# Four graph layers on one core: x transposed through DRAM and VectorE blocks instead of TensorE, products that run in either TensorE tile mode, and a new order

## The chip, the cores and the metric

The kernel runs on one core of one Trainium2 chip. The metric is the device time of one launch, in microseconds (us). Three runs of the kernel before took 2814.39, 2812.9 and 2817.28 us, so the median is 2814.39 us. Engines are named as the profile names them: PE is TensorE (its weight loads are PEld), DVE is VectorE, ACT is ScalarE, POOL is GpSimd and SP is SyncE. A small q behind a name (SPq, POOLq) is the engine's own instruction queue, from which DMAs are issued.

## What is computed

There are 32 independent graphs. Each has 512 nodes with 256 features (x) and a dense 512 x 512 adjacency (adj). Four layers follow each other, each with a residual and a layer norm. All arithmetic is float32.

```python
# layer 0: two-layer MLP on the aggregated neighbours
h = (1 + eps) * x + adj @ x
x = layernorm(x + relu(h @ W1 + b1) @ W2 + b2)
# layer 1: graph attention, 4 heads of 64, edges where adj > 0.5
h = x @ W                                    # [n, heads, 64]
e = leaky_relu(e_dst[i] + e_src[j], 0.2), masked
x = layernorm(x + softmax(e) @ h + bias)
# layer 2: 8 heads of 32, scores weighted by adj
q, k, v = x @ Wq.T, x @ Wk.T, x @ Wv.T
x = layernorm(x + softmax(q k^T / sqrt(32) + log(adj + 1e-6)) @ v @ Wo.T + bo)
# layer 3: bilinear similarity, one head
x = layernorm(x + softmax((x @ W) x^T * adj, masked) @ x)
```

## The kernel before

`fast_path` writes the whole computation as named **steps** and lets a small planner put them in order. `prepare()` makes the steps for the weights, `graph(g)` those of one graph, several hundred of them. A step has an engine, an expected duration, the steps it follows, the buffers it takes, and for TensorE a tile mode: "" (the whole array), "row" (32 rows at a time), "c32" (four column strips of 32), "r64". `Plan.order` is a list scheduler. It keeps one time line for each engine, adds `CHANGE[mode]` when a TensorE step has another mode than the step before it, and picks the ready step with the earliest due time. Due times come from a period per graph and from a long table of shifts per step name (the arguments of `plan.run`, under `tc.manual_schedule()`). What comes out is one fixed order of instructions for each engine; on the chip every engine works through its own list and waits on semaphores. The list of a graph in the middle is the same for each graph, shifted by one period, and about four to five graphs are under way at a time, each in another layer.

DMAs are steps too. A step on SP or POOL issues the transfer, a second step occupies a planned transfer queue, and a third adds the landing time. The planner has separate queues for the transfers issued from SP ("q1") and those issued from POOL ("qa"); in it the two do not touch each other.

**Buffers** are shared pools of SBUF tiles: 13 large ones ("B"), 12 of 2 x 512 floats in each partition ("C"), 10 strips ("D"), and 8 PSUM banks ("p"). The tokens L0 to L3 limit how many graphs may be inside a layer (1, 2, 2 and 1).

The steps that matter here, with their lines in the profile:

- Layer 0: `h` (L812) aggregates neighbours, `f` (L835) and `y` (L854) are the two products of the MLP. The adjacency of every graph but the first is loaded already cut into 32 x 32 blocks by four DMAs from SP (L719, tile `Ar`, 128-byte pieces), and DVE then transposes the blocks (L778). So a transpose through DMA and DVE is in use for adj already.
- `residual_steps` adds a product to x and takes the statistics (DVE, L681, L624, L625); `norm_steps` finishes the layer norm: POOL raises the variance to -0.5 (L647), DVE makes the shift (L655), and ACT scales (steps `r1` to `r4`, L670).
- Layers 1, 2 and 3 begin with **x transposed** (features first): for each of two halves TensorE makes four 128 x 128 transposes into a PSUM bank (L882 for layer 1, L1147 in `features_first` for layers 2 and 3), and ACT copies the bank into SBUF (L886, which also sums each feature over the nodes, and L1151).
- Layer 1 then has `v1` (L903), the attention weights on ACT and DVE (L1010, L1021), the products `o1` in mode c32 (L1043), the denominators (L1081) and the small transposes `yt` (L1110, L1111).
- Layer 2 has `q` and `k` (L1166), `v2` (L1184), the scores `s` in mode row (L1203), exponentials on ACT (L1216), their weighting on DVE (L1225) and `n` in mode c32 (L1261). To sum the denominators, POOL issues accumulating DMAs that add one 1 MB tile of weights to another (`collect`, L1236, steps `cd`, six a graph, and two half-size ones, L1289, step `fd`). The product `d2` (L1308, mode r64) needs the last of them; `p` (L1385) is the output product.
- Layer 3 has `i` (L1412), `t` (L1427) and `w` (L1456).
- `bias_steps` (L611) lets POOL add the biases to x by an accumulating DMA of 512 KB, three a graph. At layers 1 and 2 it comes after the transposes that read x.

Of the kernel before, what the change touches and what calls it, by code (L numbers as in the profile page):

```python
# [16 lines left out]
P = 128  # L17
# [6 lines left out]
H1 = 4  # L24
# [24 lines left out]
class Plan:  # L49
# [12 lines left out]

    CHANGE = {"": 0.207, "row": 0.218, "c32": 0.143, "c64": 0.161, "r64": 0.166}
# [69 lines left out]
    def order(self, period, ahead, window, stay, rush=(), moves=(), edges=(0, (), 0, ())):  # L133


        room = {b: [(0.0, i) for i in range(n)] for b, n in self.stock.items()}
        engine, mode, out, last = {}, "", [], 0.0
        held = [{} for _ in self.steps]
        ends = [{} for _ in self.steps]
        waits = [{n: len(s.after) for n, s in steps.items()} for steps in self.steps]  # L140
        fwaits = [[len(after) for _, after in frees] for frees in self.frees]
        ready, low, opened = {}, 0, 0
        todo = [len(steps) for steps in self.steps]
        moved = dict.fromkeys((n for steps in self.steps for n in steps), 0.0)
        turn = [max(g - 1, 0) for g in range(len(self.steps))]
        for i, early in enumerate(rush):
            turn[-1 - i] -= early
        for n, far in moves:
            moved[n] += far
        lead, tail = edges[0], len(self.steps) - edges[2]  # L150
        early, late = dict(edges[1]), dict(edges[3])

        def shift(g, name):
            return moved[name] + (early if g <= lead else late if g >= tail else {}).get(name, 0.0)

        def near(low):
            fill, until, between, left, drain = ahead
            return fill if low < until else drain if low >= len(self.steps) - left else between

        def open_to(n):  # L160
            nonlocal opened
            while opened < min(n, len(self.steps)):
                for name in self.steps[opened]:
                    if not waits[opened][name]:
                        ready[opened, name] = self.ready(opened, name, ends)
                opened += 1

        open_to(window)
        while low < len(self.steps):
            found = []  # L170
            for (g, name), t in ready.items():
                s = self.steps[g][name]
                t = max(t, engine.get(s.eng, 0.0))
                change = self.CHANGE[s.mode] if s.eng == "pe" and s.mode != mode else 0.0
                for k, (kind, _, rest) in enumerate(s.take):
                    r, n = room[kind], sum(b[0] == kind for b in s.take[:k])
                    if len(r) <= rest + n:
                        break
                    t = max(t, r[n][0])
                else:  # L180
                    due = turn[g] * period - self.left[g][name] + shift(g, name) + stay * change
                    found.append((t, due, g, name, change))
            if not found:
                return math.inf, out
            first = min(found)[0] + near(low)
            _, t, g, name, change = min((due, t, *f) for t, due, *f in found if t <= first)
            s = self.steps[g][name]
            t += change
            if s.eng == "pe":
                mode = s.mode  # L190
            del ready[g, name]
            got = {}
            for kind, key, _ in s.take:
                got[key] = held[g][key] = (kind, room[kind].pop(0)[1])
            if s.eng:
                engine[s.eng] = t + s.us
            end = ends[g][name] = t + s.us
            last = max(last, end)
            out.append((g, name, t, got))
            for h, n in s.then:  # L200
                waits[h][n] -= 1
                if not waits[h][n] and h < opened:
                    ready[h, n] = self.ready(h, n, ends)
            for k in s.frees:
                fwaits[g][k] -= 1
                if not fwaits[g][k]:
                    key, after = self.frees[g][k]
                    kind, i = held[g].pop(key)
                    free = max(ends[g][a] + self.HOP.get(self.steps[g][a].eng, 0.0) for a in after)
                    room[kind].append((free, i))  # L210
                    room[kind].sort()
            todo[g] -= 1
            while low < len(self.steps) and not todo[low]:
                low += 1
                open_to(low + window)
        return last, out

    def run(self, tries):

        self.link()  # L220
        best = min((self.order(*t)[0], t) for t in tries)
        assert best[0] < math.inf
        for g, name, _, got in self.order(*best[1])[1]:
            self.slot[g].update((key, i) for key, (_, i) in got.items())
            self.steps[g][name].emit()
# [3 lines left out]
def fast_path(  # L229
# [103 lines left out]


# [249 lines left out]
    def graph(g):  # L584
        plan.graph()
        slot = plan.slot[-1]
        last = g == B - 1
        t = {"g": g}
# [86 lines left out]
        def residual_steps(n, c2, after, free):  # L675


            @step(f"x{n}{c2}", "dve", 0.6, after + prev(f"x{n}", c2), free=(free,))
            def _(c2=c2):
                pair = t["x"][:, 2 * c2 : 2 * c2 + 2, :]  # L680
                nc.vector.tensor_add(pair, pair, t[f"py{c2}"])  # L681
                if c2 == 0:
                    norm_tiles(n)

            for j in range(2):

                @step(f"st{n}{2*c2+j}", "dve", 0.55, (f"x{n}{c2}",))
                def _(c=2 * c2 + j):
                    norm_stats(n, c)

# [133 lines left out]
        for f in range(HC):  # L824
# [3 lines left out]
                take=(f"p=f{f}",) + (() if f else ("B=h1T/2",)),  # L828
            )
            def _(f=f):  # L830
# [3 lines left out]
                for d in range(DC):  # L834
                    nc.tensor.matmul(  # L835
                        ph, w1_sb[:, d, blk(f)], t["hT"][:, d, :], start=(d == 0), stop=(d == DC - 1)
                    )
# [30 lines left out]
        for d in range(DC):  # L868

            @step(  # L870
                f"xt1{d}", "pe", 0.437, row("r1", NC) + prev("xt1", d),
                take=(f"p=xt1{d}",) + (() if d else ("L1", "C=xT1/1")),
            )
            def _(d=d):
                if d == 0:
                    t["xT"] = mid("xT1", [P, DC, N], "xT1")

                    t["R"] = little([P, H1 * NC + DC], "R")
                    t["xs"] = t["R"][:, H1 * NC :]
                pt = t[f"pt{d}"] = bank(f"xt1{d}", [P, N], f"xT1_t_{d}")  # L880
                for c in range(NC):
                    nc.tensor.transpose(pt[:, blk(c)], t["x"][:, c, blk(d)], ident)  # L882

            @step(f"xe1{d}", "act", 0.75, (f"xt1{d}",), free=(f"xt1{d}",))
            def _(d=d):
                nc.scalar.activation(  # L886
                    t["xT"][:, d, :], t[f"pt{d}"], AF.Copy, accum_out=t["xs"][:, d : d + 1]
                )

        bias_steps(2, row("xt1", DC))  # L890

        for c in range(NC):
# [5 lines left out]
            def _(c=c):  # L898
# [3 lines left out]
                for d in range(DC):  # L902
                    nc.tensor.matmul(  # L903
                        pv, t["xT"][:, d, blk(c)], wg_sb[:, d, :], start=(d == 0), stop=(d == DC - 1)
# [6 lines left out]
        plan.free("xT1", row("v1", NC))  # L911
# [10 lines left out]
        @step("R", "act", 0.14, ("ab",))  # L922
# [15 lines left out]
        @step("Rt", "pe", 0.11, ("R",), take=("p=Rt",))  # L938
# [214 lines left out]
        features_first(2, ("L2",))  # L1153
        bias_steps(3, row("xt2", DC))

        def proj(n, o):
            @step(
                f"{n}{o}", "pe", 1.72, row("xe2", DC) + prev(n, o) + (f"^we{n}",),
                take=(f"p={n}{o}",) + (() if o else (f"C={n}",)),
            )  # L1160
            def _():
# [3 lines left out]
                for d in range(DC):  # L1165
                    nc.tensor.matmul(  # L1166
                        pq, wT[n][:, d, blk(o)], t["xT2"][:, d, :], start=(d == 0), stop=(d == DC - 1)
                    )
# [231 lines left out]
        features_first(3, ("L3",), src="x3")  # L1400
        for o in range(DC):
# [3 lines left out]
                take=(f"p=i{o}",) + (() if o else ("C=iT",)),  # L1405
            )
            def _(o=o):
# [3 lines left out]
                for d in range(DC):  # L1411
                    nc.tensor.matmul(  # L1412
                        pq, w3_sb[:, d, blk(o)], t["xT3"][:, d, :], start=(d == 0), stop=(d == DC - 1)
                    )
# [6 lines left out]
        for c in range(NC):  # L1421

            @step(f"t{c}", "pe", 1.72, row("ie", DC) + prev("t", c), take=(f"p=t{c}",))
            def _(c=c):
                pt = t[f"pt{c}"] = bank(f"t{c}", [P, N], f"s3_{c}")
                for d in range(DC):
                    nc.tensor.matmul(  # L1427
                        pt, t["xT3"][:, d, blk(c)], t["iT"][:, d, :],
                        start=(d == 0), stop=(d == DC - 1),
                    )  # L1430
# [567 lines left out]
```

## Time and profile before

| What | us |
|---|---|
| median of three runs | 2814.39 |
| the profiled execution, its own time | 2813.72 |
| its span, first to last instruction | 2812.0 |
| PE busy | 2777.1 |
| DVE busy | 2235.4 |
| ACT busy | 1774.5 |
| POOL busy | 450.9 |
| mean granted TensorE clock | 0.997 of full speed |

The profile counts an engine as busy while it executes; issuing a DMA or waiting is not busy. The line "PE" counts modelled ends of matmuls, so that a busy PE can still have gaps for a change of tile mode. The chain of waits follows the work that ended last back to what released it. Of DMA queues, q0 carries what POOL issues (the accumulating transfers) and q1 what SP issues; both run on the same 16 DMA engines. "To landing" is the time from the issue to the semaphore that says that all data has arrived.

These are the groups that the change removes or touches, as the profile lists them (busy us, mean ns of one | idle time before them):

```profile
L1147 PE MATMUL xT_t<-ident,x 128*128 128x128 f32 x512 | 73.2, 275 | 4.3 <-ACT x L670 4.2
L1151 ACT COPY xT<-xT_t 128x512 f32<-128x512 f32 x128 | 72.8, 597 | 97.9 <-PE xT_t L1147 97.9
L882 PE MATMUL xT_t<-ident,x 128*128 128x128 f32 x256 | 33.6, 273 | 0.0
L886 ACT ACTIVATE xT<-xT_t 128x512 f32<-128x512 f32 x64 | 38.6, 630 | 0.0
```

There are 768 transposes of x by TensorE, 24 for each graph, and six copies by ACT for each graph.

### The profile page before, as it was taken

What the parts mean: (1) busy time and instruction counts of PE and PEld (TensorE: products, weight loads), DVE (VectorE), ACT (ScalarE), POOL (GpSimd) and SP (SyncE); (2) the same over time, 40 slices, a digit from 0 to 9 for tenths busy, and PEclk for the clock granted to TensorE, in tenths of its full rate; (3) what the DMA queues carried; (4) which work ended last, traced back from release to release, by engine and by line L of the source; (5) the groups of instructions that cost most, each with busy time, mean ns of one, the idle gap of its engine ahead of it and who ended that gap; (6) DMA issues with size and microseconds to landing.
All of it is one profiled execution on the core that took longest, in us unless ns stands there. A gap on an engine that the chain in (4) does not pass through costs nothing.

```text
span 2812.0 us, 41564 instructions
## 1 busy us (share of the span) xinstructions
PE 2777.1 (99%) x15540; PEld 1549.1 (55%) x15540; DVE 2235.4 (79%) x4139; ACT 1774.5 (63%) x3438; POOL 450.9 (16%) x526
## 2 busy tenths in 40 slices
PE   8999999999999999999999999999999999999998
PEld 6544565555555555555555655555555555555544
DVE  3878779877779877788877788777798777887785
ACT  3767566676666675666665666766666756666564
POOL 1111111111111111111111111111111111111110
PEclk9999999999999999999999999999999999999999
DMA  8476777667787667786677776667776677667650
GB/s 172 90 160 123 154 143 155 134 137 145 145 158 145 131 139 146 139 171 134 137 141 148 143 160 133 135 143 149 153 144 135 139 146 143 136 134 137 135 104 16
DMA packets 350055, 388.74 MB, mean 138 GB/s; under 512 B 265036, under 2 KB 304920, under 8 KB 317976
## 3 DMA queue, kind: packets, MB, share of 16 engines
q0 software_dynamic: 45568, 277.89, 51.2%
q1 hardware_dynamic: 303296, 107.86, 17.3%
q8 instruction: 124, 2.03, 0.3%
q14 instruction: 83, 0.68, 0.1%
q10 hardware_dynamic: 984, 0.28, 0.0%
HBM read 141.38 MB, written 17.08 MB: 56 GB/s over the span
## 4 chain that ended last, share of the span: by engine, by line
PE 92%; DVE 3%; DMA 2%; ACT 2%; issue 1%; POOL 0%; ACTq 0%; SPq 0%; DVEq 0%; POOLq 0%
PE s L1203 9%; PE hT_ps L812 8%; PE o_ps L1261 8%; PE o_ps L1043 8%; PE h1T_ps L835 8%; PE s L1427 8%; PE o_ps L1456 7%; PE y_ps L854 7%; PE v_ps L903 4%; PE iT_ps L1412 4%; PE qT_ps L1166 4%; PE v_ps L1184 4%; PE o2p_ps L1385 4%; PE kT_ps L1166 4%; PE xT_t L1147 2%; DMA z<-z 1%
## 5 line engine op out<-in xcount | busy, mean ns | idle before, releaser
L1216 ACT ACTIVATE z<-s 128x512 f32<-128x512 f32 x1024 | 535.5, 605 | 214.4 <-PE s L1203 208.1
L1225 DVE SCALAR_TENSOR_TENSOR z<-AT,z 128x1024 f32<-128x1024 f32 x512 | 601.3, 1213 | 13.0 <-ACT z L1216 12.6
L1236 POOL DMA_DIRECT2D z<-z x186 | 164.1, 889 | 1686.2 <-DVE z L1225 522.8
L1351 DVE RECIPROCAL rdT<-rdT 128x256 f32<-128x256 f32 x128 | 214.3, 1721 | 229.2 <-ACT rdT L1344 229.2
L1010 ACT ACTIVATE z<-R_bc,nT,S 128x512 f32<-128x512 f32 x512 | 372.6, 814 | 3.3 <-DMA R_bc<-R_dram 3.2
L1021 DVE SCALAR_TENSOR_TENSOR z<-z,T,edge 128x512 f32<-128x512 f32 x512 | 347.4, 745 | 16.4 <-ACT z L1010 16.2
L670 ACT ACTIVATE x<-x,shift,rstd 128x256 f32<-128x256 f32 x508 | 264.0, 591 | 75.9 <-DVE shift L655 74.6
L1203 PE MATMUL s<-qT,kT 32*128 32x512 f32 x2048 | 288.9, 633 | 0.4 <-ACT kT L1172 0.4
L1261 PE MATMUL o_ps<-z,v 128*32 128x512 f32 x2048 | 264.2, 600 | 3.1 <-DVE z L1225 2.1
L1456 PE MATMUL o_ps<-x,z 128*128 128x257 f32 x1024 | 240.3, 386 | 3.2 <-ACT z L1216 2.5
L1071 DVE TENSOR_TENSOR z<-z 128x1024 f32<-128x1024 f32 (+1 forms) x256 | 237.0, 951 | 4.2 <-PE o_ps L1043 2.7
L1043 PE MATMUL o_ps<-z,v 128*32 128x512 f32 x2048 | 237.2, 599 | 0.0
L835 PE MATMUL h1T_ps<-hT,w_sb 128*128 128x512 f32 x512 | 234.3, 599 | 0.0
L1456 PEld LDWEIGHTS o_ps<-x,z 128*128 128x128 f32 x1024 | 189.2, 189 | 77.9 <-issue 46.3
L1427 PE MATMUL s<-iT,xT 128*128 128x512 f32 x512 | 229.3, 599 | 0.0
L854 PE MATMUL y_ps<-w_sb,h1T 128*128 128x256 f32 x1024 | 226.6, 379 | 0.0
L624 DVE BATCH_NORM_STATS2 st<-x 128x6 f32<-128x256 f32 x508 | 211.5, 416 | 9.3
L812 PE MATMUL hT_ps<-AT,x 128*128 128x384 f32 (+2 forms) x768 | 210.7, 384 | 0.5 <-ACT AT L761 0.5
L854 PEld LDWEIGHTS y_ps<-w_sb,h1T 128*128 128x128 f32 x1024 | 194.0, 190 | 27.4 <-ACT z L1216 0.8
L647 POOL TENSOR_TENSOR rstd<-ve,nhalf 128x4 f32<-128x4 f32 (+1 forms) x131 | 141.1, 1077 | 356.8 <-DVE ve L641 347.7
L841 ACT ACTIVATE h1T<-h1T_ps,b_sb 128x512 f32<-128x512 f32 x128 | 87.9, 687 | 147.7 <-PE h1T_ps L835 147.7
L1203 PEld LDWEIGHTS s<-qT,kT 32*128 32x128 f32 x2048 | 88.7, 183 | 160.8 <-issue 74.1
(162 smaller groups left out, 3763.2 us busy)
## 6 DMA issues: line engine op xcount, KB each, us to landing
z<-z POOLq DMA_DIRECT2D x186, 1024.0 KB, 8.2
x<-biases POOLq DMA_DIRECT2D x96, 512.0 KB, 9.6
R_bc<-R_dram SPq DMA_DIRECT2D x32, 1024.0 KB, 4.6
Ar<-in_adj_dram SPq DMA_DIRECT2D x124, 256.0 KB, 7.5
z<-z POOLq DMA_DIRECT2D x62, 512.0 KB, 7.0
x<-in_x_dram SPq DMA_DIRECT2D x32, 512.0 KB, 9.0
out_dram<-x SPq DMA_DIRECT2D x31, 512.0 KB, 4.1
xs_row<-xs_dram SPq DMA_DIRECT2D x32, 128.0 KB, 5.6
```

The costliest lines, as they stand in the source:

```text
L812: nc.tensor.matmul(ph[:, cols], t["x"][:, m, blk(d)], moving, start=(k == 0), stop=(k == len(parts) - 1),)
L835: nc.tensor.matmul(ph, w1_sb[:, d, blk(f)], t["hT"][:, d, :], start=(d == 0), stop=(d == DC - 1))
L854: nc.tensor.matmul(py[:, j, :], t["h1T"][:, f, blk(2 * c2 + j)], w2_sb[:, f, :], start=(f == 0), stop=(f == HC - 1),)
L1010: nc.scalar.activation(t[f"e{h}"][:, c, :], t["Rbc"][:, h, :], AF.Relu, bias=t["nT"][:, h, c : c + 1], scale=t["S"][:, h, c : c + 1],)
L1021: nc.vector.scalar_tensor_tensor(z, z, t["T"][:, h, c : c + 1], t["edge"][:, c, :], op0=ALU.add, op1=ALU.mult)
L1043: nc.tensor.matmul(po[32 * q : 32 * q + 32, :], t["v"][:, c, hp * P + 32 * q : hp * P + 32 * q + 32], t[f"e{2*hp+q//2}"][:, c, :], start=( ...
L1203: nc.tensor.matmul(pk, t["k"][hs, o, blk(c)], t["q"][hs, o, :], start=True, stop=True)
L1216: nc.scalar.activation(t[f"E{k}"][:, j, :], t[f"ps{k}{j}"], AF.Exp, scale=QSCALE)
L1225: nc.vector.scalar_tensor_tensor(z, t["AT"][:, c, None, :].to_broadcast([P, 2, N]), ADJ_EPS, z, op0=ALU.add, op1=ALU.mult,)
L1261: nc.tensor.matmul(t[f"n{o}"][32 * j : 32 * j + 32, :], t["v2"][:, c, o * P + F2 * j : o * P + F2 * (j + 1)], t[f"E{k}"][:, j, :], start=( ...
L1427: nc.tensor.matmul(pt, t["xT3"][:, d, blk(c)], t["iT"][:, d, :], start=(d == 0), stop=(d == DC - 1),)
L1456: nc.tensor.matmul(py, t[f"z3{m}"][:, blk(c)], t["x3"][:, m, :], start=(m == 0), stop=(m == NC - 1),)
```

## The change

For 27 of the 32 graphs (all but graphs 0, 1, 29, 30 and 31, `near`), the transposes of x by TensorE and, at layers 2 and 3, the copies by ACT are gone. In their place `turned` does this at each of layers 1, 2 and 3: SP writes x (512 KB) to a scratch tensor in DRAM, waits until it has landed, and reads it back with four DMAs of 128 KB in 128-byte pieces, so that the 32 x 32 blocks stand where the transposed x wants them; DVE then transposes the blocks (two instructions of 128 x 512). At layer 1 the sums over nodes, which came with ACT's copy, are made by two ACT passes over the transposed tile (`xa`). The accumulating bias DMA of layers 1 and 2 now waits for the write to DRAM, which reads x.

The 512-column products `f`, `q`, `k`, `i` and `t` get the mode "any". The planner runs such a step in the mode that TensorE is in if that is "" or c32, and in c32 otherwise; `product` then issues either one matmul of 128 columns of weights or four of 32 columns. The order of all steps is searched anew, with a new period and new shifts.

```diff
+    EITHER = {"": "", "c32": "c32"}
...
+                into = self.EITHER.get(mode, "c32") if s.mode == "any" else s.mode
+                change = self.CHANGE[into] if s.eng == "pe" and into != mode else 0.0
...
+    def product(out, lhsT, rhs, start, stop):
+
+        if plan.mode != "c32":
+            nc.tensor.matmul(out, lhsT, rhs, start=start, stop=stop)
+            return
+        for q in range(4):
+            part = slice(32 * q, 32 * q + 32)
+            nc.tensor.matmul(out[part, :], lhsT[:, part], rhs, start=start, stop=stop)
...
+        near = g < 2 or g >= B - 3
...
+        def turned(n, more, src):
+
+            @step(f"xw{n}i", "sp", 0.45, row(f"r{n}", NC))
+            def _():
+                t[f"xd{n}"] = dram.tile([N, D], F32, tag=f"x{n}_dram", name=f"x{n}_dram_{g}")
+                nc.sync.dma_start(t[f"xd{n}"].rearrange("(c p) d -> p c d", p=P), t[src][:, :, :D])
+
+            transfer(f"xw{n}", 2.0, (f"xw{n}i",), land=2.5)
+
+            for a in range(4):
+
+                @step(
+                    f"xl{n}{a}i", "sp", 0.5, (f"xl{n}{a-1}i",) if a else (f"xw{n}",),
+                    take=() if a else (f"C=xL{n}/{2 if n == 1 else 1}",) + more,
+                )
+                def _(a=a):
+                    if a == 0:
+                        t[f"xL{n}"] = mid(f"xL{n}", [P, DC, N], f"xL{n}")
+                    nc.sync.dma_start(
+                        t[f"xL{n}"][32 * a : 32 * a + 32].rearrange("j d (b i) -> j d b i", i=32),
+                        bass.AP(
+                            t[f"xd{n}"].tensor, t[f"xd{n}"].offset + 32 * a,
+                            [[D, 32], [P, DC], [32 * D, N // 32], [1, 32]],
+                        ),
+                    )
+
+                transfer(f"xl{n}{a}", 1.0, (f"xl{n}{a}i",), land=3.0)
+
+            for d in range(DC):
+
+                @step(
+                    f"xe{n}{d}", "dve", 0.6, row(f"xl{n}", 4) + prev(f"xe{n}", d),
+                    take=() if d else (f"C=xT{n}",),
+                )
+                def _(d=d):
+                    if d == 0:
+                        t[f"xT{n}"] = mid(f"xT{n}", [P, DC, N], f"xT{n}")
+                    nc.vector.transpose(t[f"xT{n}"][:, d, :], t[f"xL{n}"][:, d, :])
+
+            plan.free(f"xL{n}", row(f"xe{n}", DC))
...
-        features_first(2, ("L2",))
-        bias_steps(3, row("xt2", DC))
+        if near:
+
+            features_first(2, ("L2",))
+            bias_steps(3, row("xt2", DC))
+
+        else:
+
+            turned(2, ("L2",), "x")
+            bias_steps(3, ("xw2",))
...
                 f"{n}{o}", "pe", 1.72, row("xe2", DC) + prev(n, o) + (f"^we{n}",),
-                take=(f"p={n}{o}",) + (() if o else (f"C={n}",)),
+                take=(f"p={n}{o}",) + (() if o else (f"C={n}",)), mode="any",
```

Layers 1 and 3 are treated like layer 2 (`turned(1, ("L1",), "x")` and `turned(3, ("L3",), "x3")`).

## The prediction

> **What bounds the kernel now.** I read the page first: busy shares, queues, the chain by engine.
>
> ```profile
> PE 2777.1 (99%) x15540; PEld 1549.1 (55%) x15540; DVE 2235.4 (79%) x4139; ACT 1774.5 (63%) x3438; POOL 450.9 (16%) x526
> ...
> q0 software_dynamic: 45568, 277.89, 51.2%
> q1 hardware_dynamic: 303296, 107.86, 17.3%
> ...
> PE 92%; DVE 3%; DMA 2%; ACT 2%; issue 1%; POOL 0%; ACTq 0%; SPq 0%; DVEq 0%; POOLq 0%
> ```
>
> TensorE bounds it: 92% of the chain. Nothing else is full, but VectorE is at 79% and the DMA engines at 51 + 17%. Then one period (a graph in the middle; columns are the stretch, its length, busy PE, PEld, DVE, ACT, POOL, clock, DMA share, GB/s):
>
> ```profile
> 1085.26:1170.52 85.26, 85.26 (x486) 47.92 (x485) 69.52 (x129) 55.02 (x108) 13.81 (x16) 1.00 0.72 145
> ```
>
> A graph costs 85.26 us: DVE works 69.5, ACT 55.0, the DMA engines 0.72 x 85.3 = 61. Then the chain in order of time (start, length, what), for the price of TensorE's parts:
>
> ```profile
> 1433.15 1.72 PE kT_ps L1166 x4
> 1434.87 0.87 PE xT_t L882 x8
> 1435.74 3.46 PE v_ps L1184 x16
> ...
> 1491.13 1.07 PE s L1203 x8
> 1492.20 1.00 PE o_ps L1261 x8
> ...
> 1494.07 3.63 PE h1T_ps L835 x8
> ```
>
> Eight transposes take 0.87 us, so one takes 0.109. A product of 512 columns is two records of 0.43, and 16 records of L1261 (four strips) take the same 1.72 elsewhere in this chain. After a change of mode, 8 records of L1203 take 1.07 where 8 x 0.107 = 0.86 is work: "row" costs 0.21 to enter, c32 0.14 (1.00 - 0.86), the whole array 0.19 (3.63 against 3.44 without a change).
>
> Last, how q1's small pieces fare. Packets, MB and share of the 16 engines: 1 us with q1 alone, then 6 us in which a load of `Ar` (issued at 2537.2) stands beside one collect (issued at 2536.2):
>
> ```profile
> q1 hardware_dynamic: 1428, 0.18, 115.7%
> ```
> ```profile
> q0 software_dynamic: 128, 1.05, 97.1%
> q1 hardware_dynamic: 36, 0.02, 1.4%
> ```
>
> Alone, q1 moves 1428 pieces of 128 bytes in a us. Beside a collect it all but stops: 36 packets in 6 us. From 2267 to 2271 the two queues take turns exactly, 102 packets of 8 KB against 103 of q1. A small piece waits for an 8 KB packet of the other queue every time.
>
> **What the Trainium skill says.** "TensorEngine Tiling (Array Packing)", Key Properties: a change of tiling mode drains the engine. The trace agrees: 0.14 to 0.21 us each. "DMA: Bandwidth & Descriptors", Queues, rings and completion order: each DMA engine goes round its queue rows packet by packet. The trace agrees (102 against 103), and shows what that means when one packet is 64 times the other. Same page, Two DMAs through the same engine are not ordered: a read of what an earlier DMA wrote must wait for its semaphore; so SP's wait between write and reads is real and holds SP's queue. "VectorE: DVE Perf Modes", The three transpose paths: VectorE transposes 32 x 32 blocks only, hence the DMA that places blocks; L778 has the same shape, 0.67 us.
>
> **The change part by part.** Sums are against the profiled execution, 2813.7 us, 0.7 below the median.
>
> *TensorE work removed.* 27 graphs x 24 transposes x 0.109 = 70.6 us. Counting modes in the two built orders, changes fall from 717 to 536: 92 fewer into the whole array (x 0.19), 44 into row (x 0.21), 45 into c32 (x 0.14): 17.5 + 9.2 + 6.3 = 33.0. Products in strips cost nothing more (1.72 either way); 0 to 0.02 per load group of four, I take 0. All of it is on the path: 103.6 us, giving 2710. That is 3.8 a graph.
>
> *ACT.* Four copies of 0.597 a graph go; the two of layer 1 become `xa`. ACT is at 65%: worth 0.
>
> *DVE.* Six block transposes of 0.67 are 4.0 a graph: 73.5 of 81.4, 90%. Covered by TensorE while their input is there; they also stop whatever is queued behind them while it is not.
>
> *DMA.* Per graph 12,288 pieces at 13 ns of one engine (115.7% x 16 us / 1428) = 10.0 us of all sixteen, and 1,536 of 1 KB (375 in 1.5 us at 96%: 61 ns) = 5.9. 61 becomes 77, that is 94% of 81.4. Nothing hides a late one: TensorE's list is fixed.
>
> *The time that each layer leaves.* I laid measured lengths along TensorE's built list and read off the work between producer and user.
>
> Layer 1. From the end of `y` (call it Y) to `v1` the list holds 24.3 us. In the trace before, the last copy of r1 ends at Y + 8.3, so the write is issued then. On DVE the last weighting (L1225, 1.2) before collect c7 (step cd7; c5 and c6 likewise) stands directly after r1's shift, r1's four copies (2.4) end 1.2 later: c7 is issued about Y + 7.2, its packets run from +1.4 (its usual delay) for 5.7, to Y + 14.3. The write gets turns only, then needs 24 of its 32 packets per engine alone (512 take 2.05 us, so 1.5), and 0.8 to land: L = Y + 16.6. At L both SP and POOL go on: four reads on q1, and on q0 the bias DMA (2.8) directly followed by collect c6 (5.4), which stands next in POOL's list. The reads' first quarter gets through, the rest waits to L + 9.7, then 3072 pieces take 2.6, landing 0.8, DVE 1.4: Y + 31.3. TensorE waits 31.3 - 24.3 = 7.0. From both sides: without rivalry the write takes 3.6, the reads 5.7 (1.4 to start, 3.5, 0.8), DVE 1.4: Y + 19, no wait; with nothing let through, 8.
>
> Layer 3. `p` to `i` holds 37.4, r3 is ready at 18.6 (ten us of L1021 stand before its shift on DVE). The write lies beside c5 and a half collect, 7.6; the reads share q1 with the next graph's `Ar`, 10,240 pieces, 1.4 + 8.9 + 0.8; DVE 1.4. 38.7 against 37.4: about 1, of which half shifts `v1` as well: 0.5 (0 to 3).
>
> Layer 2. `yt` to `q` holds 23.1; r2 takes 9.5, SP's queue is full of layer 3's reads until about 11.6, the write lands at 13.9, reads beside a bias DMA end at 20 to 22.5, DVE 1.4. 0 to 1; I take 0.
>
> Waits: 7.5 a graph x 27 = 202. Forecast 2710 + 202 = 2912. Behind the waiting transposes DVE holds layer 2's weightings and the reciprocals for `p`; with 15 us idle a period it makes that up.
>
> **Rivals.**
>
> *The DMAs hide* (ends faster). The saved 3.8 a graph stays, only layer 3's wait of about 1 counts: 2710 + 27 x 1.1 = 2740. It holds if the reads of layer 1 are not caught behind c6, for which 5.7 instead of 13.1 us is enough: Y + 24 against 24.3. For it: TensorE waited only some 50 us in all before (2797 from first to last matmul, 2745 of work and changes), and the same device works for `Ar`. Against it: `Ar` has a whole period of room, and lands in 3.9 to 17.0 us. Decided at a wait of 3.8 a graph.
>
> *Half caught.* A collect issued into running `Ar` traffic had its first packet 2.1 to 3.9 us after issue, not 1.4. If that delay lets most of the reads pass, the wait is about 2.5 + 0.5: 2710 + 81 = 2791.
>
> *DMA as the bound.* At 94% the waits of layers 2 and 3 come to 2 or 3 each and late collects keep buffers: 12 a graph, 3034.
>
> That the transposes do not leave is excluded: 648 fewer stand in the built list.
>
> **How the numbers follow.** About 0.2% (5.6 us) is what can be told from no change. Forecast (2850 to 2970): 0.48. Hidden (2700 to 2775): 0.29. Half caught (2775 to 2850): 0.15, split 0.06 faster, 0.04 same, 0.05 slower. Bound (over 2970): 0.08. Faster 0.35, same 0.04, slower 0.61. Both signs are likely, so the range reaches from most of "hidden" to the top of the forecast: 2728 to 2965, leaving out 0.09 below and 0.10 above. The forecast's own range is 2850 to 2970.
>
> **What would show it.** PE groups for transposes of x down to 120 instructions; busy PE minus waits near 2700; DMA share per period near 0.85; PE waits at `v_ps` of layer 1 (released by ACT or DVE behind the reads) of some 7 us a graph; reads of layer 1 landing 10 us or more after issue, of layer 2 in about half that. It is wrong if those reads land in 6 us, or if TensorE's waits gather at another step.

## The result, and the profile after

The changed kernel takes 3065.81 us (median of 4 runs, 3063.36 to 3073.78) against 2813.64 us before: a ratio of 1.090, interval 1.0877 to 1.0923. It is 252 us slower. The forecast, 2912, had the direction and the place, but its range ended at 2965, and the loss is 2.6 times the 98 us that it meant.

From the page of the changed kernel: busy time by engine, the queues, the chain by engine.

```profile
PE 2765.9 (90%) x18576; PEld 1472.5 (48%) x18576; DVE 2319.2 (76%) x4301; ACT 1731.0 (56%) x3330; POOL 475.0 (16%) x526
...
q0 software_dynamic: 45568, 277.89, 48.4%
q1 hardware_dynamic: 683024, 192.82, 28.2%
...
PE 33%; DMA 26%; DVE 24%; SPq 7%; ACT 6%; issue 2%; POOL 2%; DVEq 0%; ACTq 0%; POOLq 0%
```

TensorE's share of the chain fell from 92% to 33%; transfers and VectorE stand there now. Its busy time fell by only 11 us, though 104 us of work left its list. Both are clues: it waits, and some of what it does takes longer.

Where it waits, from the list of waits (waiting instruction, what came last, us in all, times, longest):

```profile
PE v_ps L978 <- DVE xT L740: 179.9, 24, 9.9
PE s L1284 <- ACT qT L1253: 17.2, 24, 0.9
PE d_ps L1156 <- DVE rd_all L1549: 12.1, 23, 0.9
```

The first is the wait that was forecast, `v1` behind the layer-1 reads, 7.5 us each. The other two were not in my sum.

The chain in order of time around one such wait; in this period `y` ends at 1546.6, so `v1` starts at Y + 32.9:

```profile
1554.60 2.08 ACT x L682 x4
...
1556.70 8.03 DMA x_dram<-x
...
1564.88 0.56 SPq L721
...
1568.15 10.34 DMA xL<-x_dram
...
1578.68 0.72 DVE xT L740
...
1579.54 6.66 PE v_ps L978 x16
```

The write takes 8.0 us (8.3 forecast), and from the issue of the first read to VectorE's start it is 13.8 (from the write's landing on, 13.1 forecast). What the reads meet can be counted: packets of the two queues, MB and share of the 16 engines, from 1572 to 1575:

```profile
q0 software_dynamic: 78, 0.64, 102.0%
q1 hardware_dynamic: 78, 0.01, 4.4%
```

For each of c6's packets of 8 KB one piece of 128 bytes gets through; beside the bias DMA, which comes in packets of 4 KB, it is much the same (42 against 41 from 1568.5 to 1569.5).

The last line of the chain is new: 16 matmul records of `v1` take 6.66 us; before the change they took 3.76. The windows say why (stretch, length, busy PE, PEld, DVE, ACT, POOL, clock, DMA share, GB/s): the whole period, the wait, and `v1` itself.

```profile
1546.60:1641.10 94.50, 85.61 (x595) 45.67 (x594) 73.58 (x136) 53.67 (x103) 14.94 (x16) 0.95 0.83 167
1571.50:1579.50 8.00, 1.09 (x6) 0.61 (x4) 0.81 (x2) 2.35 (x5) 0.82 (x1) 0.72 0.97 205
1579.50:1586.20 6.70, 6.66 (x17) 5.28 (x18) 6.01 (x8) 1.99 (x6) 0.00 (x0) 0.56 0.78 158
```

This period is 94.50 us long, where it was 85.26. During the wait the DMA engines are at 97%, and TensorE's granted clock falls to half and stays there through most of `v1` (0.56). Over the whole run the clock stood at half for 276 us, before the change for 18.

### The profile page after: what moved, and what is told of

Its sections match the earlier page's. It is cut to its first block, busy times and chain, and to the rows that moved or that the text cites. A ratio compares the mean times of both kernels' runs of the same rounds, so it can differ in the third digit from the quotient of the medians.

```text
span 3063.9 us, 48491 instructions
## 1 busy us (share of the span) xinstructions
PE 2765.9 (90%) x18576; PEld 1472.5 (48%) x18576; DVE 2319.2 (76%) x4301; ACT 1731.0 (56%) x3330; POOL 475.0 (16%) x526
## 4 chain that ended last, share of the span: by engine, by line
PE 33%; DMA 26%; DVE 24%; SPq 7%; ACT 6%; issue 2%; POOL 2%; DVEq 0%; ACTq 0%; POOLq 0%
DMA xL<-x_dram 13%; DMA x_dram<-x 12%; DVE z L1096 9%; PE v_ps L978 5%; SPq L721 4%; PE hT_ps L867 4%; PE o_ps L1342 4%; PE s L1284 4%; DVE z L1306 3%; DVE z L1146 3%; ACT x L682 3%; DVE st L636 2%; SPq L774 2%; PE v_ps L1265 2%; PE o2p_ps L1466 2%
## 5 line engine op out<-in xcount | busy, mean ns | idle before, releaser
L1306 DVE SCALAR_TENSOR_TENSOR z<-AT,z 128x1024 f32<-128x1024 f32 x512 | 610.1, 1214 | 130.6 <-ACT z L1297 130.4
L740 DVE STREAM_TRANSPOSE xT<-xL 128x512 f32<-128x512 f32 x162 | 106.2, 691 | 330.0 <-DMA xL<-x_dram 308.7
L978 PE MATMUL v_ps<-wg_sb,xT 128*128 128x264 f32 x512 | 174.3, 510 | 182.7 <-DVE xT L740 179.9
L1317 POOL DMA_DIRECT2D z<-z x186 | 171.0, 919 | 1042.9 <-PE o_ps L1342 587.0
L659 POOL TENSOR_TENSOR rstd<-ve,nhalf 128x4 f32<-128x4 f32 (+1 forms) x131 | 166.8, 1275 | 686.3 <-DVE ve L653 634.2
L1342 PE MATMUL o_ps<-z,v 128*32 128x512 f32 x2048 | 251.6, 596 | 7.5 <-DVE z L1306 7.4
L1118 PE MATMUL o_ps<-z,v 128*32 128x512 f32 x2048 | 241.9, 603 | 6.8 <-ACT z L1297 4.3
L978 PEld LDWEIGHTS v_ps<-wg_sb,xT 128*128 128x128 f32 x512 | 130.2, 262 | 228.0 <-issue 189.7
L1539 PE MATMUL o_ps<-x,z 128*128 128x257 f32 x1024 | 233.5, 380 | 2.4 <-ACT z L1526 2.4
L1146 DVE TENSOR_TENSOR z<-z 128x512 f32<-128x512 f32 (+1 forms) x256 | 231.1, 953 | 1.6
L344 PE MATMUL s<-iT,xT 128*32 128x512 f32 x1840 | 210.3, 594 | 0.0
```

Source lines behind the costliest of these rows:

```text
L978: nc.tensor.matmul(pv, t["xT1"][:, d, blk(c)], wg_sb[:, d, :], start=(d == 0), stop=(d == DC - 1))
L1146: nc.vector.tensor_add(z[:, :m, :], z[:, :m, :], z[:, m : 2 * m, :])
L1306: nc.vector.scalar_tensor_tensor(z, t["AT"][:, c, None, :].to_broadcast([P, 2, N]), ADJ_EPS, z, op0=ALU.add, op1=ALU.mult,)
L1342: nc.tensor.matmul(t[f"n{o}"][32 * j : 32 * j + 32, :], t["v2"][:, c, o * P + F2 * j : o * P + F2 * (j + 1)], t[f"E{k}"][:, j, :], start=( ...
L1539: nc.tensor.matmul(py, t[f"z3{m}"][:, blk(c)], t["x3"][:, m, :], start=(m == 0), stop=(m == NC - 1),)
```

## The experiments

Theory A: the layer-1 reads starve beside the large packets of POOL's queue, and TensorE's wait for them, with the slow clock behind it, is the loss. Rivals: the traffic of all three trips is the loss; the new order or the strips are.

**Layer 2 alone, planned anew.** `TURN` holds only 2; the line is put in likewise for layers 2 and 3.

```diff
-        if near:
+        if near or 1 not in TURN:
```

> Only layer 2 goes through DRAM; layers 1 and 3 are transposed on TensorE as before, products in either mode, order planned anew by the same rules. The built list of TensorE is shorter than before's by 216 transposes (23.5 us) and 122 mode changes (23.4 us): 47 us. The list holds 27 us between the last transpose of y and the first product on the turned x, and the trip of layer 2 took 22 to 23 us. Theory A (the loss is the wait for layer 1's reads, plus what it drags behind it): no wait of size is left, the clock stays at 1.00: 2813 - 47 = about 2767 (2755 to 2785). Rival B (the new order or the products in strips cost time by themselves): no faster than 2813, and product groups longer than 0.43 us a pair of records. Rival C (any DRAM trip delays the engine): waits at q or k of 3 us or more a graph, 2800 to 2850.

Measured: 3552.5 us, ratio 1.264 (1.2618 to 1.266). None of the theories. The shifts of due times had been fitted to another set of steps, and I take the order that came out to be poor in many places; no run shows that by itself. The two largest of its waits:

```profile
PE hT_ps L869 <- issue: 113.1, 18, 6.3
PE xT_t L939 <- ACT x L684: 65.3, 76, 3.3
```

Neither has to do with layer 2's trip, which TensorE waited for only 15.4 us in 24 graphs. It tells nothing on the change, except that a shorter built list isn't a faster kernel. In all further kernels the order of the kernel after (in the last one that of before) is kept and edited by hand.

**Work in the wait.**

```diff
+                if c == 0 and not near:
+                    for _ in range(18):
+                        nc.tensor.matmul(pv, w1_sb[:, 0, :P], wg_sb[:, 0, :], start=True, stop=True)
```

> As the kernel after, but 18 more matmuls of 128x264 (8.0 us at full clock, operands long there, result overwritten) stand directly before v1 of layer 1 in each turned graph, that is in TensorE's wait. The work of the kernel is unchanged, TensorE is just not idle. In the trace of after the clock stands at 0.5 for 276 us in all, always from the end of this wait on, and v1 takes 6.7 us instead of 3.6. Theory A (idle TensorE loses its clock, and this doubles the work behind it): mean clock 0.99 or more, v1 back to 3.6 us, 27 x 3.0 to 3.5 us less, minus up to 0.5 a graph where the added work reaches past the wait: 2970 to 2995. Rival (the half clock has another cause, such as load or DMA traffic): the clock stays at 0.95 to 0.96, time 3066 or more.

Measured: 3050.53 us (1.0824 to 1.086 of before), clock 0.989. From its chain, the added work and `v1`:

```profile
1573.59 8.01 PE v_ps L980 x36
1581.60 3.56 PE v_ps L982 x16
```

`v1` is back to 3.56 us. Its group before, after the change and here:

```profile
L903 PE MATMUL v_ps<-wg_sb,xT 128*128 128x264 f32 x512 | 122.1, 391 | 0.0
L978 PE MATMUL v_ps<-wg_sb,xT 128*128 128x264 f32 x512 | 174.3, 510 | 182.7 <-DVE xT L740 179.9 <-ACT xT L941 2.0 <-ACT z L1297 0.8
L982 PE MATMUL v_ps<-wg_sb,xT 128*128 128x264 f32 x512 | 122.2, 390 | 6.1 <-DVE xT L741 4.8 <-ACT xT L942 1.3
```

So the slow clock cost 52 us. The time fell by only 15, because the added work (216 us) is longer than the waits it filled (180): 52 - 36 = 16. The cause of the slow clock is shown: TensorE's idling in the wait. My 2970 to 2995 had two sizes wrong, 3.0 to 3.5 us a graph for the slow clock where it is 2.2 in 24 graphs, and at most 0.5 for the surplus where it is 1.3. The clock falls inside the wait, too, and not at its end.

**The bias DMA and c6 behind the reads.** A small add on POOL waits for the reads; in the order, POOL's steps from the bias DMA on move behind them.

```diff
+                if k == 2 and not near:
+                    w8 = little([P, 4], "w8")
+                    nc.gpsimd.tensor_tensor(w8, t["xL1"][:, 0, :4], t["xL1"][:, 0, :4], op=ALU.add)
```

> As the kernel after, but on POOL's queue a small add that reads the landed layer-1 reads stands before layer 1's bias DMA, so that this DMA and collect c6 behind it are issued after the reads have landed instead of beside them. Theory A (the reads, 128 bytes a piece, starve beside 8 KB packets of the bias DMA and c6): from issue to landing of the four reads about 6 us instead of 13, DVE done about Y + 26, wait at v1 from 8 to about 2 us a graph, less half clock: 2830 to 2890; collect c6 comes some 6 us later and could give back 1 or 2 us at d2. Rival B (the trip is as slow alone, by its bytes or by the write before it): reads still 12 us or more, 3050 to 3070. Rival C (the delay only moves to c6 and its users): v1's wait goes, but waits at d2 or p of layer 2 take its place, 3000 or more.

Measured: 3121.03 us (1.1077 to 1.1114), slower than the change itself. From issue of the first read to VectorE's start now 5.9 us (median of 19 graphs), 13.9 in the kernel after; `v1` starts at Y + 25.7 instead of Y + 32.9. So the reads did starve in that company. But the largest wait of TensorE is now:

```profile
PE d_ps L1401 <- DMA z<-z: 211.0, 23, 10.0
```

`d2` needs the fold, which stands behind c6 on POOL. In a graph that I followed, it took 33.8 us from c7's issue to the end of the fold instead of 27.7. Rival C holds for the time: this queue had no room to give.

**Large pieces.**

```diff
-                            [[D, 32], [P, DC], [32 * D, N // 32], [1, 32]],
+                                [[DC * N, 32], [1, DC * N]],
```

> As the kernel after, but layer 1's four reads take whole 4 KB rows (128 pieces instead of 4096 of 128 bytes; same bytes, same queue, same neighbours), so that layer 1's transposed x holds the wrong elements. Theory A (it is the number of turns that a small piece needs beside 8 KB packets): each engine has 8 packets instead of 256 to place, reads land 4 to 6 us after issue although the bias DMA and c6 run beside them, wait at v1 0 to 2 us a graph, 2800 to 2870. Rival B (bytes or bandwidth: DMA engines are full at that place): wait unchanged, 3040 to 3070. Rival D (the small pieces are slow by themselves, 3.5 us for 4096, not starved): only 2 or 3 us a graph come back, 2960 to 3000.

Measured: 2975.36 us (1.0561 to 1.0596). Reads: 7.6 us from the first issue to VectorE's start instead of 13.9, with the same bytes beside the same neighbours. TensorE's two largest waits:

```profile
PE d_ps L1398 <- DMA z<-z: 46.6, 19, 4.9
PE v_ps L987 <- DVE xT L749: 36.6, 18, 5.4
```

The wait at `v1` shrank by 143 us, and a third of that came back at `d2`, which is the next to be late. The starvation is confirmed from a second side (pieces, not bytes); the total is 105 us above my upper end, a first sign that not all of the loss is at `v1`.

**Layer 1 back on TensorE, order kept.** Eight transposes stand ahead of `v2` in 23 graphs.

```diff
+                for d in range(DC):
+                    for c in range(NC):
+                        nc.tensor.transpose(pts[d][:, blk(c)], t[src][:, c, blk(d)], ident)
```

> The order of the kernel after is kept instruction by instruction; only layer 1's trip is taken out again in the 23 graphs where banks allow it, and eight TensorE transposes (0.87 us) with two ACT copies stand in front of v2's products instead. Mode changes stay at 537; the list gets 23 x 0.87 = 20 us longer. From after's trace: work and changes of its list 2640, excess (waits and slow clock) 405, of it 238 at v1. Theory A (layer 1's trip is what is lost, the rest of after's excess stays as it is): 2660 + 405 - 238 x 23/27 + 16 outside = about 2878 (2860 to 2900). Rival B (the loss is spread over all three trips and their DMA load): 2950 or more. Rival C (without layer 1's trip the kernel is as fast as my sum said, about 2735): the rest of the excess would have to be a consequence of layer 1's wait.

Measured: 3083.15 us (1.0946 to 1.0983). By the letter that is rival B (2950 or more), but not for B's reason. TensorE's largest wait:

```profile
PE d_ps L1472 <- DMA z<-z: 125.9, 23, 6.9
```

My own edit did it: the bias DMA adds to the x that the transposes read, so on POOL it waited for them, and c6 stood behind it. It was issued 16.2 us after c7 (median), not 9.5. A step was moved, and the queue that waits for it was not. It is mended further down.

**The bias DMA behind the fold.**

```diff
+                i, j = at[g, "xd2"], at[g - 2, "fd1"]
+                    order.insert(j + 1, order[i])
+                    del order[i]
```

> As after, but POOL issues layer 1's bias DMA behind collect c6 and the fold after it, not directly ahead of c6. The reads of layer 1 then meet only c6 (5.4 us of 8 KB packets) instead of bias DMA and c6 (8.2 us). Theory A (reads land when the other queue's packets are through): DVE starts 2.8 us earlier than after's Y + 32.1, the wait at v1 falls from 7.5 to about 4.7 a graph: 2975 to 2995, and c6 and the fold come no later. Rival (reads are slow for another reason, or the fold takes the bias DMA's place): DVE at Y + 31 or later, 3045 to 3070.

Measured: 3004.79 us (1.0665 to 1.0701), 61 us faster than the change. Reads to VectorE: 11.0 us instead of 13.9, that is 2.9 less where 2.8 was expected. The summed wait at `v1` fell from 180 to 110 us, 2.9 a graph:

```profile
PE v_ps L986 <- DVE xT L748: 109.6, 23, 7.7
```

The mechanism holds to a tenth of a us. The time is 10 us above my range: the shorter wait is followed by half clock as well (mean clock 0.966), so nothing came back beyond the wait, and 9 of the 70 us I have not traced.

**Nobody waits for the reads (flawed).**

```diff
-                    nc.vector.transpose(t[f"xT{n}"][:, d, :], t[f"xL{n}"][:, d, :])
+                    nc.vector.transpose(t[f"xT{n}"][:, d, :], w1_sb[:, d, :])
```

> As after with every DMA of the three trips, but VectorE's block transposes read a weight tile that is always there instead of the landed reads (so the turned x holds wrong numbers): nobody waits for a trip any more, the DMA traffic and VectorE's work are unchanged. Theory A (latency of the trips and the slow clock behind it is the loss, the traffic itself is covered): list 2640 + waits like those of before (47) + the new small waits of the order (some 50) + 16 = about 2750 (2735 to 2790), faster than before. Rival B (the traffic of the trips slows collects or other loads, and that is the loss): 2850 or more, with waits at d2 or at h.

Measured: 2943.53 us (1.0431 to 1.0476). It did not do what it was made for. ACT's waits show that `v1`'s copies, whose tile takes over the buffer of the reads, still waited for them:

```profile
ACT v L984 <- DMA xL<-x_dram: 68.7, 14, 6.4
```

By the letter that is rival B, but I draw nothing from it; the next three do its work.

**No trips at all.**

```diff
+                return
                 t[f"xd{n}"] = dram.tile([N, D], F32, tag=f"x{n}_dram", name=f"x{n}_dram_{g}")
...
+                    return
                     if a == 0:
```

> As e7_no_latency, and the writes and reads of the three trips are left out as well. Theory A: the traffic costs nothing beyond the latency: within 10 us of e7_no_latency. Rival B (traffic costs): faster than e7 by 20 us or more.

Measured: 2777.37 us, ratio 0.9871 (0.9854 to 0.9887). It is 166 us faster than e7_no_latency, by the letter rival B; but as e7's copies still waited for the reads, the two together don't part traffic from latency. The run by itself says what the removed transposes, strips and new order are worth when every trip is free: 36 us, not the 104 of my sum. TensorE's two largest waits:

```profile
PE s L1286 <- ACT qT L1255: 17.3, 24, 1.1
PE d_ps L1158 <- DVE rd_all L1551: 11.5, 23, 0.5
```

They are in the kernel after too, hardly in the one before (0.4 and 0.5 us in all). In the new order the scores follow directly on `q`'s product, whose ACT copy they need, and layer 1's denominators come before VectorE's last sum for them is done. From start to start they cost 0.8 us (2.61 from `q` to the scores, where 1.85 is usual) and 1.0 us (with the small transposes behind them), 42 us together. Two groups of scores in a row take 2.34 us in 23 graphs and 1.93 in the last: 9 us more, whose cause I don't know. The other 17 of the missing 68 I have not traced.

**Which trip.** First `FREE` holds layer 1, so that the other two trips are real; then it holds 2 and 3.

```diff
+                if n in FREE:
+                    return
```

> As after, but only layer 1's trip is taken away: its write and reads are left out and VectorE transposes a weight tile instead (wrong numbers). Layers 2 and 3 make their real trips, with their traffic and their latency. e8_no_trip_dma, the same without any trip, took 2777. Theory A (layer 1's trip is the one that is late; those of layers 2 and 3 have room in the middle of the run): 2777 + some 40 for the first and last graphs, whose i and k waited 30 us for layers 2 and 3 in after: 2800 to 2835. Rival B (the traffic of layers 2 and 3 delays collects and loads too): 2860 or more.

Measured: 2848.23 us (1.0109 to 1.0142), 71 more than without any trip: between A's upper end (2835) and B's lower one (2860), about as far from either. A period in the middle is 84.1 us against 83.5 without trips. Most of the rest is at the ends of the run; the longest waits (12.9, 11.0 and 10.8 us) lie at 330, 2378 and 2670 us:

```profile
PE kT_ps L341 <- DVE xT L745: 17.1, 2, 12.9
...
PE kT_ps L345 <- DVE xT L745: 13.0, 6, 11.0
...
PE iT_ps L341 <- DVE xT L745: 10.8, 1, 10.8
```

> The reverse: layers 2 and 3 are taken away (no write, no reads, VectorE transposes a weight tile; wrong numbers), layer 1 makes its real trip. Theory A (the reads of layer 1 starve beside the bias DMA and c6, whoever else is on q1): wait at v1 6 to 8 us a graph and half clock behind it, 2777 + 27 x 8 to 10 = 2990 to 3050. Rival B (all three trips together fill q1 and the DMA engines): wait at v1 3 us or less, 2830 to 2900.

Measured: 2982.73 us, ratio 1.0604 (1.0586 to 1.0622), 205 more than without trips and 7 under A's range. Most of the wait at `v1` (179.9 us in the kernel after) is still there:

```profile
PE v_ps L985 <- DVE xT L745: 149.8, 24, 8.3
```

`v1` starts at Y + 31.5 though no other trip runs. So it is layer 1's trip beside POOL's transfers, not the sum of all trips; that its reads starve there is what the runs before show. The two prices add up: 2777 + 71 + 205 = 3053 against 3066 measured with all three.

**Layer 1 back on TensorE, mended:** the edits of e5_layer1_undone and e6_bias_last together, and banks for the transposed x that no one needs soon:

```diff
-            return left
+            return sorted(left, key=lambda s: -later[s])
```

> e5_layer1_undone with its flaw mended: there the bias DMA had to wait on POOL for the late transposes that read x, and held collect c6 and the fold behind it, so d2 waited 126 us. Here the bias DMA is issued after c6 and the fold; the transposed x gets banks that nobody needs soon; 24 graphs of 27 are undone. Theory A: 2777 + 24 x 0.87 + 3 graphs with their old wait (30) + first and last graphs (40): about 2868 (2835 to 2890), no wait at d2. Rival B (d2 waits anyway, as the fold chain is slow beside the trips of layers 2 and 3): 2950 or more.

Measured: 2901.08 us, ratio 1.0308 (1.0291 to 1.0326), 11 above the range. `d2` waits 0.4 us in all, so e5's flaw was what I took it for. It is the fastest kernel of this study that still computes the reference with trips in it, and it is 89 us slower than before. Keeping the order of after, even free trips give 2777, 1.3% under before; I found no version that beats both kernels.

**Strips alone,** in the order of the kernel before:

```diff
+            s = self.steps[g][name]
+            if s.eng == "pe":
+                self.mode = self.EITHER.get(self.mode, "c32") if s.mode == "any" else s.mode
```

> The kernel before, in its own order, with its transposes; only the 512-column products take four strips of 32 columns where the instruction ahead of them left TensorE in that mode: 288 products run in strips (eight matmuls for two), mode changes 729 against 718 and nearly the same in price (129.9 against 130.7 us by the costs of each kind). My sum took strips at the price of the whole array (1.72 us a product). If that holds: 2813 within 5 us. Rival (a strip costs more to start, by 0.02 us for each group of four): 288 x 4 x 0.02 = 23 us more. Rival (strips alone are worth something without the new order): 2800 or less.

Measured: 2819.64 us (18 runs) against 2813.19, ratio 1.0022 (1.0014 to 1.0029): 6.5 us more, just outside the first expectation. Divided by 288 products it would be 0.02 us each, but the traces don't put it there. Windows of this run (the first graphs, then one period in the middle) and of the kernel before (the first graphs):

```profile
86.20:231.30 145.10, 135.11 (x844) 67.84 (x841) 115.43 (x197) 92.94 (x185) 25.05 (x26) 0.94 0.64 128
1103.60:1188.75 85.15, 85.15 (x610) 45.37 (x602) 69.47 (x128) 55.06 (x108) 13.84 (x16) 1.00 0.74 144
```
```profile
86.10:225.20 139.10, 131.91 (x783) 67.39 (x780) 115.47 (x196) 92.61 (x185) 25.92 (x26) 0.99 0.66 133
```

In the middle a period with strips is 0.1 us shorter than before (85.15 against 85.26). The first graphs take 6.0 us longer: TensorE waits 4.1 us for a copy of `k` there, where it was 0.4, and the clock is at 0.94. So strips cost nothing in the steady part, and without the new order they save next to nothing.

## Why the prediction was right in kind and wrong in size

*TensorE work removed: right.* Laid out start to start, work and changes of mode come to 2744.0 us before and 2639.7 after, 104.3 less where I had 103.6. Strips at the price of the whole array were right too: 85.15 us a period with them, 85.26 without (e12_strips_only). A product is four records of 0.43 us, not two as I wrote; its price, 1.72, was the right one.

*"All of it is on the path": the first step that failed.* The work left the list, but two new waits of 0.8 and 1.0 us a graph came in, and in e8_no_trip_dma only 36 of the 104 us remain. Both can be read from the built order: a consumer so close behind its producer that the ACT copy or the VectorE sums between them take longer than what TensorE has left to do. I looked in that order only for the distances around the trips.

*Layer 1: mechanism right, wait close.* I had DVE done at Y + 31.3 (my terms add up to 31.1); `v1` starts at Y + 32.9. Against the kernel without trips (Y + 24.9) the wait is 8.0 us, forecast 7.0. The order of events was the forecast one too: write beside c7, then reads beside bias DMA and c6. Reads without these neighbours take 5.9 us (5.7 forecast), beside c6 alone 11.0, beside both 13.9. One of the lines that led me there I had misread: from 2537 to 2543, 20 of q1's 36 packets belong to an earlier transfer, and the load of `Ar` itself has its first packet only at 2542.4. That window shows a late start beside a collect, not turns; the turns are in the other one (102 against 103), and in the kernel after (78 against 78). That SP must wait between write and reads rests on the page that the prediction names; no run leaves that wait out.

*What follows the wait: the second step that failed, by leaving it out.* The wait was priced at its own length. `v1` then runs for the most part at half clock and takes 5.4 to 6.9 us instead of 3.7. The Trainium skill would have told me: "TensorE: Matmul & The Clock Gate", HAM oscillation, describes a loop in which TensorE's wait for a transfer is long enough for the clock to be halved, so that each next piece of work starts slow. The trace agrees (0.56 of full clock in `v1`, 52 us in all, and none of it when the wait is filled with work).

*Layers 2 and 3: right in the middle, wrong at the ends, the third step that failed.* The forecast 0.5 a graph is 0.6. My distances were those of a graph in the middle; at the first and last turned graphs the list between `yt` and `k` or `p` and `i` runs differently, and the ends cost most of the 71 us. I had given these graphs the price of the middle.

Over the whole run the forecast missed 154 us. Of the saving 68 were gone, the slow clock took 52, layers 2 and 3 took 71 where I had 14, and the wait at `v1` was 180 where I had 189: 68 + 52 + 57 - 9 = 168. These prices were measured apart; the 14 us too many I have not traced. For one graph in the middle, in us:

| part | forecast | measured | from |
|---|---|---|---|
| work and mode changes | 81.4 | 81.4 | built list, start to start |
| new waits of the order | 0 | 2.1 | period 83.5 without trips |
| wait at `v1` | 7.0 | 8.0 | Y + 32.9 against Y + 24.9 |
| slow `v1` | 0 | 2.2 | 52 us in 24 graphs |
| layers 2 and 3 | 0.5 | 0.6 | period 84.1 against 83.5 |
| sum | 88.9 | 94.3 | the median period is 94.4 |

*ACT and DVE at no cost: right.* VectorE's busy time rose by 84 us and ACT's fell by 44, and the period of e8_no_trip_dma shows no cost of either beyond the waits named above. *DMA share:* forecast 0.85, measured 0.83.

*The rivals.* "The DMAs hide" and "half caught" fell with the wait. "DMA as the bound" (3034) had the nearest number for a wrong reason: with the trips of layers 2 and 3 alone the middle of the run loses 0.6 us a graph, not the 4 to 6 that it assumed. In one point it was nearer than my forecast: between c7 and the fold the DMA engines are full (97% in the wait). Putting the reads first made `d2` late by 211 us, and with the bias DMA last `v1` still waited 110; that no order of the two queues lets both be in time is not shown.

## What to carry to other kernels

When work leaves the bound engine for a round trip through DRAM, price the trip by pieces and by what the other queue has under way at that moment, then ask what is due from that other queue, before counting any of the saving. A wait of several us that comes back every period can cost its length and the slow clock behind it. And a new order must be read for every producer and consumer that it puts next to each other: here such waits were most of the 68 us, of 104 saved, that were gone before any transfer was late.

## What I had not expected of the hardware

The clock's loss doesn't grow with the wait. In the kernel after, 23 waits of 4.7 to 9.9 us at `v1` were each followed by a loss of 1.6 to 3.1 us (half of the time at half clock in the 12 us from `v1`'s start). With large pieces, four of the eight waits of 2.1 to 3.1 us cost nothing and four 1.7 us; the waits at `v1` below 2 us cost 0 to 0.8 there.

The size of the pieces alone moved the time of the reads of 512 KB, from issue to VectorE's start, from 13.9 to 7.6 us beside the same packets of 4 and 8 KB; with the neighbours gone the small pieces needed 5.9. So small pieces were slow here only in company.
